# A graph block on one core: byte matrices written in runs of ten, keys summed against normed rows, and a new order around the seams

## The chip, the cores and the metric

The kernel runs on one core of a Trainium2 chip. The engines are TensorE (PE, with its weight loads shown apart as PEld), VectorE (DVE), ScalarE (ACT), GpSimd (POOL) and SyncE (SP), which here only issues transfers. Each engine works through its own list of instructions in order. The metric is the device time of one execution in microseconds (us), and times are medians over several runs.

## What is computed

There are 6250 nodes with 256 features and 200000 edges, sorted by their target (dst). Cut to what matters, the reference is:

```
xn = layernorm(x)
# graph convolution with self-loops: h = xn @ W, messages scaled by dinv[src] * dinv[dst]
gnn = relu(segment_sum((xn @ W)[src] * norm, dst) + b)
# linear attention mixer: q, k, v = xn @ Wqkv, 8 heads of 32
q, k = elu(q) + 1, elu(k) + 1
kv = einsum('nshd,nshm->nhmd', k, v);  ksum = k.sum(1)
t  = q . kv / (q . ksum + 1e-6)
x1 = layernorm(t + xn);  mix = layernorm(gelu(x1 @ W1 + b1) @ W2 + b2 + x1)
x  = x + gnn + mix
# 8 experts, one per token (argmax), at most 977 tokens each, in order of token
x  = x + expert_ffn(layernorm(x))      # 256 -> 1024 -> 256, times the gate's probability
```

The sums kv and ksum run over all nodes, so the second half of the mixer can start only when the keys of all nodes are done.

## The kernel before

Nodes are handled in 49 tiles of 128 rows (the last has 106), mostly two tiles at a time (25 "pairs"). There are three stages.

**First stage.** Two generators of instructions are woven together by hand: C, the chain of lists (`first_chain`), and F, the first passes over x (`first_passes`). Before the weaving starts, the statistics of the first eight tiles are placed (`all_of(x_stats(8))`). Then one step of C is followed by steps of F until F has made FIRST = 0.79 steps for each step of C. The order so made is the order on every engine.

C first finds where each node's edges begin (`search`): 25 comparisons of dst against the node numbers on DVE (L433), summed by PE (L436), give a coarse place per group of nodes (L447), then POOL fetches windows of dst (L454), in which DVE and ACT count (L466, L470). It needs dst alone, except that it pulls the statistics of x along. From the degrees follows dinv. Then C scales the rows of x in place (L403), splits them into a high and a low part in a table in SBUF (`tab`, L394 and L396) and writes them to memory (g_dram), and beside that builds the edge lists. At its end it adds up a few checks (`checked`).

F, per pair: ACT makes the normed rows (L682) out of x, which for the first NX = 6 pairs is read where it was loaded, and for the others is loaded once more (L673); PE turns them (L242); queries (L708), `ex` and `re` (elu + 1) and a write to memory (q_dram); then per tile keys and values in one product of 512 columns (L721), elu + 1 of the keys (L726, L728, L732), a copy of the values beside a column of ones (L730), and the outer product of keys and values, 129 columns for each half of the keys, summed in PSUM over all tiles (L694). It also fills the experts' buffer with zeros (L660, L661). Float32 products show as two records each in the profile, fp32r and bf16 ones as one.

After both, DVE masks the summed outer products by head (kvb), and a flag from the checks is loaded into all engines; a branch on it leads to a slow general path, which is not taken with these inputs.

**Aggregation.** Three generators are woven: `gather` (618 steps: 18 node tiles whose edges' rows POOL gathers from memory, L984, and PE adds up by one-hot products, L1002), `dense` (31 node tiles, in 13 steps each), and `rounds` (the rest of the block per pair, up to routing), which makes SIDE = 1.25 steps for each step of `gather`. A round waits for the sums of its pair.

`dense` counts edges in a matrix of 128 targets by 6272 sources per node tile. One-hot products (L967) give, in PSUM, 10 targets by 49 blocks of sources at a time; ACT casts them to bytes (L969), 403 times, into a tile [128, 128, 49] (place of the source in its block on the partitions, target, block), that is, 490 bytes in a row. The multiplication with the table needs one block of sources at a time, [128, 128]: ACT takes seven blocks (`widened`, L927, 217 times), reading bytes that lie 49 apart, into fp32r, and PE multiplies (L952).

In `rounds`, `routing` works once for two pairs: among others a running count over tiles on DVE (`fore`, L1052), two steps later a product on PE that waits for it (L1056), and at the end POOL scatters each token with its scale and its row number, 514 floats, into the experts' buffer `xbuf` (L1083).

**Experts.** The memory of the earlier stages is given back, and each expert loads its weights (1 MB each, L1332 and L1334) and its tokens (L1338: four tiles, then three, then the rest), turns the tokens (L1351), and does its two products (L1367, L1377). DVE copies out the row numbers (`who`, L1343), ACT multiplies by the scale (L1380), and POOL scatters the rows to the output (L1395). The loads of the first two experts are issued ahead of the first product.

## Time and profile before

| | |
|---|---|
| time, median of 8 runs | 1853.55 us (1845.24 to 1857.96) |
| profiled execution | 1855.44 us, of which its span 1853.3 us |
| PE busy | 1503.6 us (81%), granted clock 0.904 |
| DVE, ACT, POOL busy | 1087.7, 1040.6, 772.6 us |
| DMA | 286.41 MB, mean 155 GB/s |

A busy time is the time in which an engine has an instruction in work; PE's ends are modelled. The span is cut here by what the engines do: the first stage runs until 273 us, where the last outer product ends; the aggregation from the first one-hot at 281 us until the last table product at 1478 us; the last round and its routing follow, and the experts from 1518 us on.

### The profile page before, as it was taken

How to read it: one execution, taken by the hardware profiler on the slowest of the kernel's cores; microseconds unless marked ns; L12 is line 12 of the kernel's file. 1: busy time of each engine (PE TensorE's matmuls, PEld its weight loads, DVE VectorE, ACT ScalarE, POOL GpSimd, SP SyncE). 2: the span in 40 equal slices, each digit the busy share in tenths (PEclk: the TensorE clock that was granted, in tenths of full speed). 3: DMA queues.
4: the chain of work that ended last, by engine and by line, in shares of the span. 5: the costliest groups of instructions: out<-in, count | busy, mean ns of one | idle time of the engine just before them, and what ended most of it. 6: DMA issues, size and time to landing. Idle time of an engine off the chain costs nothing. (4 is left out here: it accounts for less than half of the span.)

```text
span 1853.3 us, 23596 instructions
## 1 busy us (share of the span) xinstructions
PE 1503.6 (81%) x7678; PEld 1085.5 (59%) x7678; DVE 1087.7 (59%) x3430; ACT 1040.6 (56%) x1639; POOL 772.6 (42%) x771
## 2 busy tenths in 40 slices
PE   4887786887877887888778888788888739999997
PEld 2554454665655665666556666566656526777775
DVE  4765856676676577667666767666766322223323
ACT  1844554767666676677557666666766413242332
POOL 0103506556546565555555555555655411111111
PEclk9988996999889998899889898888988859999999
DMA  7546787657556566565656565565665462332330
GB/s 224 152 123 190 240 265 183 161 154 189 141 155 161 153 169 178 145 168 149 169 155 166 148 169 159 148 159 159 156 158 143 119 221 103 104 108 102 109 105 21
DMA packets 184985, 286.41 MB, mean 155 GB/s; under 512 B 28457, under 2 KB 78564, under 8 KB 184714
## 3 DMA queue, kind: packets, MB, share of 16 engines
q0 software_dynamic: 96304, 180.15, 37.7%
q1 hardware_dynamic: 88250, 103.44, 17.1%
q8 instruction: 69, 1.13, 0.2%
q10 hardware_dynamic: 288, 1.08, 0.1%
q14 instruction: 74, 0.61, 0.1%
HBM read 226.90 MB, written 60.39 MB: 155 GB/s over the span
## 5 line engine op out<-in xcount | busy, mean ns | idle before, releaser
L984 POOL DMA_INDIRECT gt<-g_dram,idxc x612 | 622.5, 1017 | 548.4 <-PE ps L1002 296.5
L952 PE MATMUL ps_d<-tab,A_r 128*128 128x512 f32 x1519 | 453.7, 423 | 36.2 <-ACT A_r L927 25.7
L927 ACT CAST A_r<-A 128x896 fp32r<-128x896 uint8 x217 | 391.5, 1804 | 78.2 <-PE ps_d L952 50.2
L952 PEld LDWEIGHTS ps_d<-tab,A_r 128*128 128x128 f32 x1519 | 309.5, 205 | 116.8 <-ACT A_r L927 36.7
L969 ACT CAST A<-bp 128x490 uint8<-128x490 f32 (+1 forms) x403 | 221.1, 562 | 258.8 <-PE bp L967 133.4
L1002 PE MATMUL ps<-gt,oh 128*128 128x512 f32 x612 | 287.0, 504 | 6.8 <-DMA gt<-g_dram,idxc 5.8
L899 DVE TENSOR_TENSOR lo<-rowb,lo 128x640 bf16<-128x640 bf16 (+1 forms) x403 | 193.5, 480 | 137.0 <-PE bp L967 48.4
L967 PE MATMUL bp<-hi,lo 128*128 128x98 bf16 x1984 | 169.0, 217 | 41.8 <-DVE hi L899 20.3
L967 PEld LDWEIGHTS <-lo 128*128 128x128 bf16 x1984 | 108.3, 103 | 159.2 <-issue 86.1
L993 DVE TENSOR_TENSOR oh<-rowb,rel 128x256 fp32r<-128x256 bf16 x306 | 128.2, 419 | 106.0 <-PE ps L1002 73.4
L1395 POOL DMA_INDIRECT out<-rep,who x43 | 42.4, 986 | 300.7 <-DVE rep L1393 202.0
L899 DVE TENSOR_TENSOR hi<-hib,hi 128x490 bf16<-128x490 bf16 (+1 forms) x403 | 163.1, 405 | 0.0
L1367 PE MATMUL hpf<-xet,w1e 128*128 128x512 f32 (+2 forms) x544 | 151.5, 436 | 5.6 <-ACTq L1407 3.5
L1377 PE MATMUL ypf<-w2e,hm 128*128 128x256 f32 (+1 forms) x688 | 151.3, 379 | 0.0
L1377 PEld LDWEIGHTS ypf<-w2e,hm 128*128 128x128 f32 (+1 forms) x688 | 128.9, 188 | 21.9 <-issue 3.1
L1002 PEld LDWEIGHTS ps<-gt,oh 128*128 128x128 f32 x612 | 117.6, 208 | 13.6 <-DMA gt<-g_dram,idxc 6.1
L1367 PEld LDWEIGHTS hpf<-xet,w1e 128*128 128x128 f32 x544 | 85.5, 191 | 65.3 <-issue 57.4
L1369 ACT ACTIVATE hm<-hpf,fb_s 128x512 f32<-128x512 f32 (+2 forms) x136 | 71.0, 525 | 78.4 <-PE hpf L1367 73.9
L1379 DVE TENSOR_TENSOR y<-ypf,fb_s 128x256 f32<-128x256 f32 (+1 forms) x43 | 18.2, 423 | 140.1 <-PE ypf L1377 140.1
L721 PE MATMUL mm<-wqkv_s,xnt 128*128 128x512 f32 (+1 forms) x196 | 98.8, 629 | 0.0
L1380 ACT ACTIVATE y<-y,xe 128x256 f32<-128x256 f32 (+1 forms) x43 | 21.9, 508 | 119.4 <-DVE y L1379 119.4
L1206 ACT ACTIVATE s<-s,nb,rs 128x256 f32<-128x256 f32 (+1 forms) x98 | 53.5, 595 | 49.5 <-DVE nb L1200 18.9
(307 smaller groups left out, 2074.3 us busy)
## 6 DMA issues: line engine op xcount, KB each, us to landing
g_dram<-tab SPq DMA_DIRECT2D x24, 512.0 KB
xt<-in_x SPq DMA_DIRECT2D x42, 256.0 KB
xbuf<-zeros SPq DMA_DIRECT2D x26, 384.0 KB
gt<-g_dram,idxc POOLq DMA_INDIRECT x612
xe<-xbuf SPq DMA_DIRECT2D x8, 1028.0 KB
w1e<-in_fw SPq DMA_DIRECT2D x8, 1024.0 KB
w2e<-in_fw SPq DMA_DIRECT2D x8, 1024.0 KB
xe<-xbuf SPq DMA_DIRECT2D x8, 771.0 KB
```

The costliest lines, as they stand in the source:

```text
L721: nc.tensor.matmul(kp[:r, :], xnt[:, c, i * r:i * r + r], wqkv_s[:, c, D:3 * D], start=(c == 0), stop=(c == 1))
L899: V.tensor_tensor(one[:, :g1 - g0, :].rearrange("p g (w t) -> p g w t", t=2), row.rearrange("p (w t) -> p w t", t=2).unsqueeze(1).to_broad ...
L927: nc.scalar.copy(o, mats[u][:, :, c * CH:(c + 1) * CH].rearrange("p n s -> p s n"))
L952: nc.tensor.matmul(acc_ps, parts[u - 1, hi // CH][:, hi % CH, :], source(hi), start=False, stop=(hi == NB - 1))
L967: nc.tensor.matmul(bp[:, g * HI:(g + 1) * HI], lo[:, g, :], hi[:, g, :], start=(g == 0), stop=(g == g1 - g0 - 1))
L969: nc.scalar.copy(mats[u][:, GN * g0:GN * g1, :].rearrange("p n s -> p (n s)"), bp[:, :(g1 - g0) * HI])
L984: nc.gpsimd.indirect_dma_start(out=gt, out_offset=None, in_=g_dram, in_offset=bass.IndirectOffsetOnAxis(ap=idxs[j // IC][:, j % IC:j % IC ...
L993: V.tensor_tensor(oh, rowb.unsqueeze(1).to_broadcast([P, 2, P]), rel[:, m:m + 2].unsqueeze(2).to_broadcast([P, 2, P]), op=OP.is_equal)
L1002: nc.tensor.matmul(ps, ohs.pop(i), tiles.pop(i), start=False, stop=(e == EB - 1))
L1367: nc.tensor.matmul(hp[:, :nn], w1e[:, c, f * P:(f + 1) * P], xet[:, c, at:at + nn], start=(c == 0), stop=(c == 1))
L1369: nc.scalar.activation(hm[:, f, :nn], hp[:, :nn], AF.Relu, bias=fb1_s[:, e * 8 + f:e * 8 + f + 1])
L1377: nc.tensor.matmul(yp[:r, :], hm[:, f, (i - i0) * P:(i - i0) * P + r], w2e[:, f, :], start=(f == 0), stop=(f == DFF // P - 1))
```

## The change

- **Bytes.** The byte matrix becomes [128, 49, 128] (place in the block, block, target). The cast out of PSUM (L969 before) reads 10 values that lie 49 words apart and writes them as a run of ten bytes, 49 runs for one cast; the widening cast (L927 before) reads seven blocks in a row.
- **Mixer sums.** F multiplies keys alone (256 columns, two tiles in one bank), so that exp, relu and elu + 1 of the keys are one operation each per pair. The outer product is taken of keys with the normed rows and a column of ones (257 columns, `kx_ps`, two banks). After the last pair the sum is copied, turned, multiplied with the values' weights, and masked. Normed rows have three buffers of their own and are made two pairs ahead; the turn of the next pair stands in F's first step. F has three steps per pair instead of five.
- **Order of the first stage.** The first nine steps of C (ALONE) stand ahead of the statistics of the first eight tiles. FIRST is 0.465. x is read in place for 18 pairs, so 7 pairs instead of 19 are loaded again.
- **Flag and first loads.** The checks are added up when C ends, and the flag is loaded two steps of F later. The loads of the first two rounds are made by a function of their own, `load_round`; it is called for them twice. In the order that results, on every engine the branch comes right behind F, and the turning and multiplying of the sum stands behind the branch, ahead of the aggregation's first one-hots.
- **Routing** has one step more between the running count and the product that needs it. SIDE is 1.28.
- **Experts** live where the table was (`big` now outlasts the stages): weights in its first two parts, tokens in the next two, the middle layer in the last two. The first expert's weights are asked for as soon as `gather` and `dense` are done. Tokens come ahead of weights, for the first expert tile by tile; scales and row numbers come by loads of their own, 8 bytes a row (`xm`).

```
-SIDE = 1.25
-NX = 6
-FIRST = 0.79
+SIDE = 1.28
+NX = 18
+ALONE = 9
+FIRST = 0.465
...
-    kv_ps = kps.tile([P, 2, 132], F32, name="kv_ps")
+    kx_ps = kps.tile([P, 2, 512], F32, name="kx_ps")
     cr_ps = rps.tile([P, 512], F32, name="cr_ps")
-    sm_ps = rps.tile([P, 512], F32, name="sm_ps")
+    sm_ps = cr_ps[:, 128:]
...
-            xn = pair("S", 2, "xn")
+            xn = xns[gi % 3]
...
-        def outer(t, r, ek, va):
-            for g in range(2):
-                nc.tensor.matmul(kv_ps[:, g, :129], ek[:r, g * P:(g + 1) * P], va[:r, g, :],
-                                 start=(t == 0 and g == 0), stop=(t == NB - 1 and g == 1))
+        def outer(gi, ek):
+            t0, n = twos[gi]
+            r = rows(t0)
+            for i in range(n):
+                for g in range(2):
+                    nc.tensor.matmul(kx_ps[:, g, :D + 1], ek[:r, i, g * P:(g + 1) * P], xns[gi % 3][:r, i, :],
+                                     start=(t0 + i == 0), stop=(t0 + i == NB - 1))
...
-            re = pair("G", 3, "re")
+            re = pair("S", 2, "re")
             nc.scalar.activation(re[:, :, :nn], qp[:, :, :nn], AF.Relu)
-            xn = normed(gi + 1) if gi + 1 < NGR else None
+            if gi + 1 < NGR:
+                turned(gi + 1, xns[(gi + 1) % 3])
             yield
             V.scalar_tensor_tensor(ex[:, :, :nn], ex[:, :, :nn], 1.0, re[:, :, :nn], op0=OP.min, op1=OP.add)
             nc.sync.dma_start(q_dram[gi, :, :, :nn], ex[:, :, :nn])
+            kp = bank().rearrange("p (t o) -> p t o", t=2)
             for i in range(n):
-                kp = bank()
                 for c in range(2):
-                    nc.tensor.matmul(kp[:r, :], xnt[:, c, i * r:i * r + r], wqkv_s[:, c, D:3 * D],
+                    nc.tensor.matmul(kp[:r, i, :], xnt[:, c, i * r:i * r + r], wqkv_s[:, c, D:2 * D],
                                      start=(c == 0), stop=(c == 1))
...
+            if late:
+                outer(*late.pop())
+            ek = rw.tile([P, 2, D], F32, name="ek", tag="ek", bufs=2)
+            nc.scalar.activation(ek[:r, :n], kp[:r, :n], AF.Exp)
+            rk = pair("S", 2, "rk")
+            nc.scalar.activation(rk[:r, :n], kp[:r, :n], AF.Relu)
+            if gi + 2 < NGR:
+                normed(gi + 2)
+            yield
+            V.scalar_tensor_tensor(ek[:r, :n], ek[:r, :n], 1.0, rk[:r, :n], op0=OP.min, op1=OP.add)
+            late.append((gi, ek))
+            yield
...
+    def load_round(k):
+        if k < len(twos):
+            gi = order[k]
+            t0, n = twos[gi]
+            r = rows(t0)
+            round_x[gi] = pair("X", 3, "xt")
+            nc.sync.dma_start(round_x[gi][:r, :n, :], node_rows(x, t0, n))
+            round_q[gi] = pair("Q", 2, "q")
+            nc.sync.dma_start(round_q[gi][:, :, :n * r], q_dram[gi, :, :, :n * r])
...
+        for _ in range(ALONE):
+            next(C)
+        all_of(x_stats(8))
+        while any(live):
+            if live[1]:
+                live[1] = next(C, "end") != "end"
+                c += 1
+                if not live[1]:
+                    badi = judged()
+                    asked = f + 2
+            while live[0] and (f < FIRST * c or not live[1]):
+                live[0] = next(F, "end") != "end"
+                f += 1
+                if not live[1] and f == asked:
+                    flag = nc.values_load(badi[0:1, 0:1], min_val=0, max_val=1)
+        assert f > asked
+        for k in range(2):
+            load_round(k)
+
+        kx = pair("S", 2, "kx")
+        nc.scalar.copy(kx, kx_ps[:, :, :D])
+        kxt = pair("S", 2, "kxt").rearrange("p c (g m) -> p c g m", g=2)
+        tp = bank()
+        for g in range(2):
+            V.tensor_scalar(kvb[:, g, 128:132], hmask[:, :, 0], kx_ps[:, g, D:D + 1], None, op0=OP.mult)
+            for c in range(2):
+                nc.tensor.transpose(tp[:, (2 * c + g) * P:(2 * c + g + 1) * P], kx[:, g, c * P:(c + 1) * P], ident)
+        nc.scalar.copy(kxt.rearrange("p c g m -> p (c g m)"), tp)
+        kv = bank()
+        for g in range(2):
+            for c in range(2):
+                nc.tensor.matmul(kv[:, g * P:(g + 1) * P], kxt[:, c, g, :], wqkv_s[:, c, 2 * D + g * P:2 * D + (g + 1) * P],
+                                 start=(c == 0), stop=(c == 1))
+            V.tensor_tensor(kvb[:, g, 0:128], kv[:, g * P:(g + 1) * P], hmask.rearrange("p a b -> p (a b)"), op=OP.mult)
+        for k in range(2):
+            load_round(k)
...
-                    nc.scalar.copy(o, mats[u][:, :, c * CH:(c + 1) * CH].rearrange("p n s -> p s n"))
+                    nc.scalar.copy(o, mats[u][:, c * CH:(c + 1) * CH, :])
...
-                        mats[u] = de.tile([P, P, NB], U8, name="A", tag="A")
+                        mats[u] = de.tile([P, NB, P], U8, name="A", tag="A")
...
-                        nc.scalar.copy(mats[u][:, GN * g0:GN * g1, :].rearrange("p n s -> p (n s)"), bp[:, :(g1 - g0) * HI])
+                        nc.scalar.copy(mats[u][:, :, GN * g0:GN * g1],
+                                       bp[:, :(g1 - g0) * HI].rearrange("p (n s) -> p s n", s=NB))
...
             yield
+            yield
             yield
             pp = bank()
...
+            if not (alive["g"] or alive["d"] or weights):
+                weights.append(weights_of(0))
...
-            for i0, i1 in ((0, 4), (4, NCT - 1)):
+            parts = [(i, i + 1) for i in range(4)] if e == 0 else [(0, 4)]
+            for i0, i1 in parts + [(4, NCT - 1)]:
                 nc.sync.dma_start(xe[:, i0:i1, :],
-                                  xbuf[r0 + i0 * P:r0 + i1 * P, :].rearrange("(t p) d -> p t d", p=P))
...
+            w1e, w2e = weights.pop() if e == 0 else weights_of(e)
+            nc.sync.dma_start(xm[:, :NCT - 1, :], xbuf[r0:i1, 2 * D:].rearrange("(t p) d -> p t d", p=P))
+            nc.sync.dma_start(xm[:last, NCT - 1, :], xbuf[i1:r0 + CAP, 2 * D:])
```

## The prediction

> **What bounds the kernel now.** I read the windows of busy time by stage first, then who waits for whom in the longest stage, then the groups of instructions by shape, then the order of time at the seams. By stage (start and end, length, then busy us and count on PE, its weight loads, DVE, ACT and POOL, granted clock, DMA share, GB/s):
>
> ```profile
> 0.00:23.00 23.00, 0.00 (x0) 0.08 (x1) 11.65 (x78) 1.69 (x2) 3.21 (x18) 1.00 0.77 237
> 23.00:50.00 27.00, 25.46 (x109) 12.58 (x108) 12.09 (x30) 9.03 (x22) 0.00 (x0) 1.00 0.69 203
> 50.00:145.00 95.00, 80.18 (x315) 51.76 (x314) 71.19 (x276) 59.92 (x162) 6.92 (x7) 0.91 0.44 133
> 145.00:273.00 128.00, 101.31 (x406) 66.04 (x406) 85.15 (x248) 72.27 (x181) 43.88 (x42) 0.91 0.77 246
> 273.00:282.00 9.00, 0.07 (x1) 0.01 (x1) 1.51 (x8) 0.49 (x2) 0.00 (x0) 0.54 0.17 45
> 282.00:1478.00 1196.00, 973.28 (x5462) 720.64 (x5462) 800.30 (x2512) 786.59 (x1055) 670.59 (x656) 0.89 0.61 159
> 1478.00:1520.00 42.00, 8.85 (x36) 6.78 (x36) 11.16 (x55) 2.83 (x6) 5.60 (x5) 0.59 0.55 195
> 1520.00:1853.00 333.00, 314.48 (x1355) 227.58 (x1353) 94.62 (x228) 107.74 (x211) 42.39 (x43) 0.99 0.28 97
> ```
>
> Four parts: the lists and the first passes (0 to 273), PE idle for 23 us and 81% busy from 50 on; aggregation (282 to 1478), where PE is 81%, DVE 67% and ACT 66% busy, so none is full and each waits in its own order for the others; a tail (to 1520) in which the routing's last scatter and the first load of tokens stand alone; the experts, PE 94% busy at clock 0.99. In the aggregation PE waited (us in total, times, longest):
>
> ```profile
> PE mm L242 <- ACT s L1206: 31.2, 16, 4.3
> PE mm L1056 <- DVE fore L1052: 28.6, 11, 3.5
> ...
> PE ps_d L952 <- ACT A_r L927: 25.7, 18, 5.9
> ...
> PE mm L1238 <- ACT x1t L1220: 7.9, 5, 2.5
> ```
>
> The groups that the change touches there, with two DVE rows for comparison (busy us, mean ns; the tile's row of L886 has min/median/max ns):
>
> ```profile
> L927 ACT CAST A_r<-A 128x896 fp32r<-128x896 uint8 x217 | 391.5, 1804 | 78.2 <-PE ps_d L952 50.2 <-remote 11.7 <-PE bp L967 10.0
> L969 ACT CAST A<-bp 128x490 uint8<-128x490 f32 x372 | 206.5, 569 | 214.0 <-PE bp L967 104.7 <-PE ps L1002 46.1 <-remote 44.8
> ```
>
> ```profile
> L886 DVE TENSOR_REDUCE ag<-ps_d x31: 682/691/692, 342.8 to 1478.0; 128x256 f32<-128x512 f32 x31
> ```
>
> ```profile
> L1281 DVE TENSOR_TENSOR s<-mm,s 128x512 f32<-128x512 f32 x24 | 16.5, 687 | 8.4 <-PE mm L1272 8.4
> ```
>
> L927, reading bytes 49 apart, costs 1804 ns for 896 elements; L394, a contiguous ACT cast of 512 elements, costs 628.
>
> **The change, part by part.** The sum is made against the profiled execution, 1855.4 us (span 1853.3); the median shown is 1.9 lower.
>
> *First stage, head.* From the order of time:
>
> ```profile
> 15.80 0.43 DVE L374 BATCH_NORM_STATS2 six<-x_in 128x6 f32<-128x256 f32 x1 [9.58 <-DMA x_in<-in_x]
> ...
> 22.79 0.76 DVE L433 TENSOR_SCALAR lt<-reps,lastf 125x784 bf16<-125x784 int16 x2
> 23.27 2.14 PE L436 MATMUL et_ps<-lt,oneb 125*1 125x448 bf16 x6 [23.27 <-DVE lt L433]
> ```
>
> ```profile
> 50.05 0.17 DVE L447 TENSOR_SCALAR at<-cr_ps 112x7 f32<-112x7 f32 x1 [2.43 <-PE cr_ps L445]
> ```
>
> The search needs only dst, whose loads are issued before those of x. When they land no view shows: between 2.5 us (issue) and 15.8 (x, behind them, was there). I take 8: dst's 0.8 MB stand ahead of the first 1 MB of x, and 237 GB/s move both in 7.6. 25 steps at the 0.7 us that six matmuls in 2.14 show end at 25; then DVE has its copy (0.6) and, now ahead of L447, eight tiles of statistics (6.8 from 15.8 to 22.6): L447 at 33 instead of 50, 17 us earlier.
>
> *First stage, work per pair of tiles.* From rows at 252 to 256 us:
>
> ```profile
> 254.07 1.88 PE L721 MATMUL mm<-wqkv_s,xnt 128*128 128x512 f32 x4
> ```
>
> ```profile
> 252.34 1.89 PE L708 MATMUL mm<-xnt,wqkv_s 128*128 128x256 f32 x8
> ...
> 255.78 0.61 PE L694 MATMUL kv_ps<-va,ek 128*128 128x129 f32 x4
> ```
>
> Keys and values cost PE 2 x 1.88 per pair; keys alone are eight records of 256 columns, as L708: 1.89. The outer product grows from 129 to 257 columns: from 2 x 0.61 to some 1.89. Net -1.20 per pair, x 24.5 pairs = -29 us of PE, on the path: at the 81% that PE keeps from 50 on, -36. ACT loses six operations of 0.38 and gains two of 0.60 per pair (-27 in all), DVE's two of 0.42 become one of 0.69 (-4): beside PE, counted at nothing. Twelve loads of x (256 KB, 1.04 us of SP each) go; SP and DMA (0.77 busy) are not named by PE's waits, so nothing again, and if C's rows were short of them it is a gain. Against that: before, 1.5 pairs were done by 50 us, now none by 33: 1.5 x 6.2 / 0.81 = +12. And in the order of the changed program three pairs of F stand behind the end of the chain of lists, with nothing beside them: +6. In place of the row reads (x_in) DVE's in-place scaling (L403) waits for ACT's norms; these stand two pairs ahead in the order, so 0.
>
> *Seam.* 9 us lie between the last products and the first one-hot (273 to 282): flag load, branch, a barrier. The flag is now read two F steps after it is made (its load was 0.7 us). But the summed keys-times-norms must be copied, turned, copied, multiplied and masked before DVE's first one-hot: ACT 0.6, PE 0.6, ACT 0.6, PE 0.6, DVE 0.6, with handovers some 4; of this the old mask and check (1 us) and the load go away: +2. SP loads the first two rounds twice; the second set waits for the first set's buffers, and the round behind it needs them only after the chain: 0, at most 3.
>
> First stage: -17 - 36 + 12 + 6 + 2 = -33. Bounds: -3, if the chain of lists sets its end (-17 + 2.7 pairs x 6.2 alone at the end - 3 at the seam), and -45, if neither lost pairs nor lone pairs cost.
>
> *Aggregation.* L927 now reads contiguous bytes. From 256 to 512 elements ACT's copies go from 383 to 608 ns (L730, L690), 0.88 ns an element; 896 give 628 + 384 x 0.88 = 0.97 us. Bounds 0.97 and 1.80 (should the cast itself be slow; but L910 widens 128 bytes in 0.31). I take 0.97: -0.84 x 217 = -182 us of ACT's 787. L969 now reads PSUM at steps of 49 words and writes runs of ten bytes, 403 times. Bounds: 0.57, as now, and 1.07, if each of 490 elements costs what L927's do now. The nearest row by memory is L886: neighbouring reads there are 256 words apart, and its 691 ns equal L1281's 687 of contiguous PSUM. It is DVE, not ACT; still I take 0.57.
>
> [...]
>
> What reaches PE: the 18 waits for A_r shrink by up to 0.84 each: -15. The 31 waits for ACT's s, x1t, ht and agt (31.2 + 7.9 + 5.5 + 4.4 = 49.0) shrink, where a cast stands ahead, by half of that: -13. The routing's extra step: 618 gather steps in 1196 us with 1.25 round steps each make 1.55 us a step; the 11 waits for fore lose that: -17. SIDE 1.28 for 1.25 moves round steps 2% earlier; they wait for sums: 0. Together -45. Bounds: -17 (ACT buys nothing) and -95 (nearly all of the 79 us that ACT's groups end, and the fore waits). What is late next: DVE (hi, lo and ag end 40 us of PE's waits).
>
> *Tail and experts.* The last scatter took 7.10 us while 4 MB of weights were in flight (issued 1492.8 to 1501.6); these now go out near 1478 and are gone by then: 0 to -4, taken -2.5. Tokens took 5.39 us as 1 MB and come tile by tile: 0 to -5, taken -2.5. Later experts load tokens ahead of weights, and their scales and row numbers (8 bytes a row) last, behind 4 MB issued 27 us before use: DVE's who waits for them with PE's next products not behind it; 0, and if they come late, 2 us for each of six experts.
>
> Sum: 1855.4 - 33 - 45 - 5 = 1772; less 1.9, **1770**.
>
> **Rivals.**
> 1. *L969 pays for its strided read* (1.07): +206 us of ACT cancel L927's -182, and ACT's -28 is gone: 1798. For it: L927's own price. Against: L886.
> 2. *The chain of lists sets the first stage's end*, -3 instead of -33: 1800. For it: DVE is 67% busy from 145 on and the chain has DMA round trips (L449 to L466). Against: PE's 81% in the same stretch.
> 3. *ACT is the pacemaker of the aggregation*: -95 instead of -45: 1720. For: 79 us of PE's waits end on ACT. Against: ACT itself waits more for PE (105 us at L969 alone) than PE for it.
> 4. *Slower: L969 at 1.8 us*, strided read and short runs both paying. ACT then has 787 - 182 + 403 x 1.23 = 1101 us; at 88% busy the stage takes 1250, +54, which less 38 elsewhere gives 1871 (1869). It decides from 1.76 us on. Against: no ACT row costs over 2.0 ns an element, this would be 3.7.
> 5. *The cast is slow, not the stride*: L927 stays at 1.80: 1798. Against: L910, L394.
>
> **Numbers.** Chances: forecast 0.51, rivals 0.20, 0.10, 0.08, 0.07, 0.04. Runs of the kernel before differ by 0.7%, medians of several by less; 0.3% is about what tells a change from none. Rivals 1 to 3 and 5 are faster; 4 is slower. Of the 0.93 of the faster cases I give 0.02 to no change and 0.01 to slower, for several misses at once: faster 0.90. The range runs from rival 3 to rival 1 or 2 with something of the other: 1722 to 1818; left out are rival 4, both of 1 and 2, and the far side of 3, some 0.15. The forecast's own range is 1750 to 1792.
>
> **What would show it.** Right: L447's counterpart at 31 to 37 us; last outer product near 240; first one-hot near 249; the A_r cast at 0.97 and the A cast at 0.57; waits for fore near 1 us each; aggregation near 1150 long; first token transposes some 35 us after its end. Wrong, above all, if the A cast comes out at 1 us or more, or if the chain of lists ends the first stage later than 250.

## The result and the profile after

The changed kernel took 1835.35 us (median of 12 runs, 1824.68 to 1843.59), the kernel before 1851.91 in the same comparison (33 runs): ratio 0.991, 95% interval 0.989 to 0.993. The forecast was 1770 with a range of 1722 to 1818, so the sign was right and four fifths of the gain did not come: 83 us were forecast (1853.55 - 1770), 16.6 came. The profiled execution took 1833.1 us, span 1831.2.

In some comparisons the kernel before took 1852 to 1856 us (called here the first condition), in others 1731 to 1734 (the second), and one and the same chip showed both, so a ratio is taken within one comparison and traces are compared within one condition. The traces of before and after are of the first, the pair c_before and c_after further below of the second.

The stages of the changed kernel, first condition (start and end, length, then busy us and count on PE, its weight loads, DVE, ACT and POOL, granted clock, DMA share, GB/s):

```profile
0.00:23.00 23.00, 7.53 (x29) 2.67 (x30) 11.66 (x66) 1.28 (x1) 3.21 (x18) 1.00 0.77 234
...
36.00:126.00 90.00, 70.37 (x310) 58.17 (x310) 69.25 (x265) 56.88 (x126) 6.95 (x7) 0.87 0.41 126
126.00:241.00 115.00, 85.47 (x371) 70.56 (x372) 76.56 (x218) 61.30 (x124) 43.81 (x42) 0.87 0.76 241
241.00:264.00 23.00, 18.47 (x85) 15.29 (x83) 8.75 (x22) 8.19 (x18) 0.00 (x0) 0.93 0.60 191
...
272.40:1451.80 1179.40, 973.82 (x5462) 722.92 (x5462) 800.79 (x2513) 615.49 (x1055) 672.38 (x656) 0.89 0.63 164
1451.80:1489.00 37.20, 8.16 (x28) 5.72 (x28) 10.67 (x54) 2.50 (x5) 5.62 (x5) 0.54 0.28 94
1489.00:1831.20 342.20, 318.38 (x1360) 229.32 (x1360) 92.89 (x221) 108.32 (x211) 42.50 (x43) 0.97 0.30 99
```

The early marks came earlier, the first of them about as forecast: the search ends at 35.5 us (forecast 33), the row weights stand at 126.0 instead of 145.3, and the chain of lists ends at 240.4 instead of 266.0. But the last outer product ends at 263.6 instead of 273.0: for 23 us F runs alone behind the chain, where it was 7 before. The first one-hot comes 9.0 us earlier. ACT lost 171 us of work in the aggregation (786.6 to 615.5), which got 17.4 us shorter, PE's own 973 us being the same. The tail up to the first product of an expert is 0.7 shorter, and the experts from that product on are 5.0 longer (338.0). The sum is -9.0 - 17.4 - 0.7 + 5.0 = -22.1, the difference of the spans.

The two casts came out as the forecast took them (ACT's groups in the aggregation):

```profile
L1023 ACT CAST A<-bp 128x490 uint8<-128x490 f32 x372 | 217.0, 590 | 317.2 <-PE bp L1021 157.7 <-PE ps L1057 70.8 <-remote 51.9
L981 ACT CAST A_r<-A 128x896 fp32r<-128x896 uint8 x217 | 204.1, 941 | 83.1 <-PE ps_d L1006 49.3 <-remote 19.7 <-PE ps L1057 7.3
```

L981 at 941 ns (forecast 970, before 1804), L1023 at 590 (569 before). PE's waits in the aggregation, and two of ACT's (us in total, times, longest):

```profile
...
PE mm L243 <- ACT s L1250: 33.2, 16, 5.5
...
PE mm L1112 <- DVE fore L1107: 18.1, 10, 2.5
...
PE mm L1211 <- ACT agt L1184: 12.3, 7, 3.5
PE ps_d L1006 <- ACT A_r L981: 10.1, 6, 2.7
```

```profile
ACT A L1023 <- PE bp L1021: 185.0, 121, 5.8
...
ACT s L1250 <- DVE nb L1244: 54.4, 16, 7.0
```

The wait for A_r fell by 15.6 us, as forecast, and the one for fore by 10.5 where 17 were forecast. The wait for s did not fall (31.2 before): ACT itself waits there, 54.4 us, for DVE's nb. What ACT gave up became idle time of ACT.

### The profile page after: what moved, and what is told of

It reads as the page before. It is cut to its first block, busy times and chain, and to the rows that moved or that the text cites. A ratio compares the mean times of both kernels' runs of the same rounds, so it can differ in the third digit from the quotient of the medians.

```text
span 1831.2 us, 23437 instructions
## 1 busy us (share of the span) xinstructions
PE 1492.0 (81%) x7690; PEld 1110.0 (61%) x7690; DVE 1082.7 (59%) x3399; ACT 856.4 (47%) x1544; POOL 774.7 (42%) x771
## 3 DMA queue, kind: packets, MB, share of 16 engines
q1 hardware_dynamic: 93846, 101.04, 17.1%
## 5 line engine op out<-in xcount | busy, mean ns | idle before, releaser
L1006 PE MATMUL ps_d<-tab,A_r 128*128 128x512 f32 x1519 | 454.4, 424 | 23.4 <-issue 13.1
L1023 ACT CAST A<-bp 128x490 uint8<-128x490 f32 (+1 forms) x403 | 231.8, 581 | 369.7 <-PE bp L1021 185.0
L1006 PEld LDWEIGHTS ps_d<-tab,A_r 128*128 128x128 f32 x1519 | 309.8, 205 | 98.3 <-issue 17.8
L953 DVE TENSOR_TENSOR lo<-rowb,lo 128x640 bf16<-128x640 bf16 (+1 forms) x403 | 193.8, 481 | 125.6 <-PE ps L1057 41.0
L981 ACT CAST A_r<-A 128x896 fp32r<-128x896 uint8 x217 | 204.1, 941 | 83.1 <-PE ps_d L1006 49.3
L953 DVE TENSOR_TENSOR hi<-hib,hi 128x490 bf16<-128x490 bf16 (+1 forms) x403 | 163.1, 405 | 0.0
L1418 PE MATMUL hpf<-xet,w_e 128*128 128x512 f32 (+2 forms) x544 | 154.3, 441 | 8.5 <-ACTq L1459 3.5
L1428 PE MATMUL ypf<-w_e,hm 128*128 128x256 f32 (+1 forms) x688 | 151.3, 379 | 0.0
L1428 PEld LDWEIGHTS ypf<-w_e,hm 128*128 128x128 f32 (+1 forms) x688 | 128.8, 188 | 22.0 <-issue 3.8
L1418 PEld LDWEIGHTS hpf<-xet,w_e 128*128 128x128 f32 x544 | 86.7, 194 | 70.5 <-issue 62.2
L1250 ACT ACTIVATE s<-s,nb,rs 128x256 f32<-128x256 f32 (+1 forms) x98 | 53.5, 594 | 74.1 <-DVE nb L1244 54.4
L1431 ACT ACTIVATE y<-y,xm 128x256 f32<-128x256 f32 (+1 forms) x43 | 21.8, 508 | 134.4 <-DVE y L1430 132.2
L1139 POOL DMA_INDIRECT xbuf<-slot,put x48 | 51.6, 1075 | 67.1 <-issue 42.9
```

Source lines behind the costliest of these rows:

```text
L953: V.tensor_tensor(one[:, :g1 - g0, :].rearrange("p g (w t) -> p g w t", t=2), row.rearrange("p (w t) -> p w t", t=2).unsqueeze(1).to_broad ...
L981: nc.scalar.copy(o, mats[u][:, c * CH:(c + 1) * CH, :])
L1006: nc.tensor.matmul(acc_ps, parts[u - 1, hi // CH][:, hi % CH, :], source(hi), start=False, stop=(hi == NB - 1))
L1023: nc.scalar.copy(mats[u][:, :, GN * g0:GN * g1], bp[:, :(g1 - g0) * HI].rearrange("p (n s) -> p s n", s=NB))
L1418: nc.tensor.matmul(hp[:, :nn], w1e[:, c, f * P:(f + 1) * P], xet[:, c, at:at + nn], start=(c == 0), stop=(c == 1))
L1428: nc.tensor.matmul(yp[:r, :], hm[:, f, (i - i0) * P:(i - i0) * P + r], w2e[:, f, :], start=(f == 0), stop=(f == DFF // P - 1))
```

## The experiments

### The lone end of the first passes: e1_first

```diff
-FIRST = 0.465
+FIRST = 0.505
```

> The changed kernel with FIRST 0.505 in place of 0.465: in the order of the program some four or five steps of the first passes are left when the chain of lists ends, instead of eleven. Theory (the lone tail): in the changed kernel the chain of lists ended at 240.4 us and the last outer product at 263.7, and those 23 us ate the gain of the first stage; here the chain ends at 245 to 250 and the last outer product at 254 to 258, -6 to -10 us, about 1827 us, 0.987 of the kernel before. Rival (the stage is full all the same, what moves out of the tail lengthens the stretch ahead of it one for one): chain end near 252, last outer product 262 to 265, time 1833 to 1837, ratio 0.990 to 0.992.

Measured in the second condition: ratio 0.981 (0.977 to 0.985), the changed kernel 0.983 there (c_after, below). The chain of lists ended at 246.8 us instead of 236.8, the last outer product at 259.6 instead of 260.0, the first one-hot at 267.2 instead of 268.6. The rival was right in kind: what moves out of the lone end lengthens the stretch ahead of it almost one for one.

### The layout of the bytes: e2_layout and b_layout

Undone in the changed kernel:

```diff
-nc.scalar.copy(o, mats[u][:, c * CH:(c + 1) * CH, :])
+nc.scalar.copy(o, mats[u][:, :, c * CH:(c + 1) * CH].rearrange("p n s -> p s n"))
...
-mats[u] = de.tile([P, NB, P], U8, name="A", tag="A")
+mats[u] = de.tile([P, P, NB], U8, name="A", tag="A")
...
-nc.scalar.copy(mats[u][:, :, GN * g0:GN * g1],
-               bp[:, :(g1 - g0) * HI].rearrange("p (n s) -> p s n", s=NB))
+nc.scalar.copy(mats[u][:, GN * g0:GN * g1, :].rearrange("p n s -> p (n s)"), bp[:, :(g1 - g0) * HI])
```

> The changed kernel with the byte matrix laid out as before (49 bytes between neighbours for the A_r cast, contiguous writes for the A cast): ACT gets some 182 us back in the aggregation, all else stays. The forecast's terms (18 waits for A_r x 0.84 = 15, other waits for ACT 13): aggregation 1207 instead of 1179, time 1863, ratio 1.006. Theory now (ACT was not what PE waited for, its relief became ACT idle time): aggregation +4 to +12, time 1839 to 1847, ratio 0.993 to 0.997. Rival (the layout alone made the whole gain of the aggregation): +17, 1852, ratio 1.000.

The same lines the other way round in the kernel before, nothing else:

> The kernel before with the new layout of the byte matrix alone (both casts), nothing else changed. Theory (the layout is the whole gain of the change where the standstills are gone; undone in the changed kernel it cost 29 us): aggregation 25 to 36 shorter than 1079, ratio 0.979 to 0.986. Forecast's terms for ACT (15 + 13): 28 shorter, ratio 0.984. Rival (it pays only together with the other edits of the aggregation): under 15, ratio above 0.991.

Measured: e2_layout 0.999 (0.997 to 1.002), second condition; against 0.983 of the changed kernel there, the layout is worth 0.0169 x 1732 = 29 us, with an uncertainty of 6 from the two intervals. b_layout 0.987 (0.983 to 0.991), first condition: 24 us, uncertain by 7. The forecast's 28 stands, and the theory made from the first pair of traces (4 to 12 us) falls. Within the errors the layout is the whole gain: in the first condition it gives 0.987 alone, where the whole change gives 0.991, and the aggregation with it alone is 1177.2 us long (279.6 to 1456.8) against 1179.4; in the second condition nothing is left without it.

### The routing's extra step: e3_route

```diff
                 V.tensor_add(fore[:, b + 1, :], fore[:, b, :], oh[:, b, :])
             yield
             yield
-            yield
             pp = bank()
```

> The changed kernel without the routing's extra step: the product over fore is issued one step of the rounds earlier. Forecast (each of 11 waits loses 1.55 us): PE's wait for fore grows from 18.1 back to 28 us or more and the time by 17: 1852, ratio 1.000. Theory now (named waits fell by 10 only, and some of that came back at other waits): +3 to +8, ratio 0.993 to 0.995. Rival (the step buys nothing, a wait only moves to the next one): within 2 us of the changed kernel, ratio 0.990 to 0.992.

Measured: 0.976 (0.972 to 0.980) against 0.983, so without the step the kernel is 11 us faster, uncertain by 8. PE's wait for fore is 20.2 us (11 times) without the step and 18.8 (11 times) with it, and 23.6 in e2_layout, which has the step and the old layout. The step does next to nothing for the wait that it was to shorten; forecast (17 us worse) and theory (3 to 8 worse) are both wrong. The traces do not show the 11 us either: the profiled executions of the two kernels took 1699.3 and 1700.7 us, as close as the rival had it.

### The distance from DVE to ACT to PE in the rounds: e4_norms

```diff
                 V.scalar_tensor_tensor(nb, mstat[:, :, 0], -1.0, rs, op0=OP.mult, op1=OP.mult)
                 yield
                 yield
+                yield
+                yield
```

> The changed kernel with two more steps of the rounds between the DVE chain that ends in nb and ACT's norms. In the changed kernel ACT waited 54.4 us for nb and PE 33.2 us for the s that these norms write (16 times each). Theory (PE's waits in the rounds are the distance from DVE to ACT to PE in the written order, not the load of any engine): both waits fall below 15 us, the aggregation shortens by 12 to 25 us, time 1811 to 1823, ratio 0.978 to 0.985. Rival (the engines are late by their load, so the wait shows up at the next handover): the wait for s falls, others grow as much, aggregation within 5 us, ratio 0.988 to 0.994. Second rival (25 rounds that are two steps longer make the tail longer): -5 to +5 with the tail some 3 us longer.

Measured: 0.962 (0.959 to 0.965), 36 us below the changed kernel, uncertain by 7: in this condition two empty steps are worth about as much as the whole change (30 us). PE's waits in the aggregation of e4_norms, then ACT's:

```profile
PE ps L1057 <- DMA gt<-g_dram,idxc: 32.2, 32, 4.1
PE bp L1021 <- DVE hi L953: 19.8, 11, 2.7
PE mm L1112 <- DVE fore L1107: 13.5, 11, 2.6
...
PE mm L243 <- ACT s L1252: 6.2, 5, 2.2
```

```profile
ACT A L1023 <- PE bp L1021: 264.0, 202, 6.0
...
ACT s L1252 <- DVE nb L1244: 28.1, 18, 3.2
```

In c_after these two waits were:

```profile
PE mm L243 <- ACT s L1250: 51.1, 37, 3.9
```

```profile
ACT s L1250 <- DVE nb L1244: 71.5, 25, 4.5
```

The aggregation of e4_norms (columns as in the stages above):

```profile
271.30:1278.90 1007.60, 893.98 (x5454) 671.35 (x5454) 795.64 (x2510) 614.19 (x1055) 681.09 (x656) 0.95 0.72 193
```

It is 1007.6 us long instead of 1046.5 (-38.9). PE idles only 11.9 less: the wait for s fell by 44.9, but the waits for gathered rows and for hi grew (14.6 to 32.2 and 8.7 to 19.8). The other 27.0 is PE's busy time (894.0 against 921.0, the same 5460 or so records), and most of that is the clock. In these traces the granted clock is either 1.0 or 0.5, and by the records of it PE lost 62 us of its busy time to half clock in c_after and 39 in e4_norms. In c_after most products with x1t took 379 ns at 1.0, and most of those at 0.5 some 634; in the first trace of the changed kernel these are the medians of the 125 that ran at 1.0 throughout and of the 62 at 0.5. Why less of the time is at half clock is not shown.

So the theory holds for the wait for s, which is a distance in the written order, and not for the wait for nb, which did not fall below 15 (28.1). The first rival is right for most of the idle time, which moved to the next handovers, and the larger part of the gain was in neither. The second rival fell: a round that is two steps longer cost next to nothing (the tail is 0.5 us longer), as a round waits in the written order until the sums of its pair are there.

### Both kernels in the second condition: c_before and c_after

Nothing is edited; the first pair had shown times in which PE, DVE and ACT stood still together, some 35 us of the aggregation in each trace.

> The kernel before, unchanged, once more with its trace: the four kernels above ran on another chip than the first two traces, with the kernel before at 1731.5 us there instead of 1852. In the traces of the first chip PE, DVE and ACT stood still together for 35 us of the aggregation with no releaser that the trace shows, in both kernels; in the traces of the other chip for 0 to 5 us. Theory (the standstills belong to the chip, not to the change): here too they are gone, the first stage is as long as on the first chip within 6 us (270 to 282 to the first one-hot), the aggregation is 1060 to 1080 instead of 1197. Rival (the changed kernel's order removes them): the kernel before shows 20 us of them here too.

> The changed kernel, unchanged, beside the kernel before on one chip, with both traces. Theory (where the standstills are gone, the layout of the bytes is worth what the forecast gave it, 28, or the 36 by which the aggregation of the kernel with the old layout was longer; the rest of the change is worth little): aggregation 1030 to 1040, ratio 0.976 to 0.982. Rival (the ratio of the first chip holds everywhere): 0.989 to 0.993.

Measured: c_after 0.983 (0.980 to 0.985), at 1700.7 us against 1733.8. Counting stretches over 0.1 us, PE, DVE and ACT stood still together for 0.1 us of the aggregation in c_before and for 2.2 in c_after, against some 35 in each trace of the first pair. So the standstills do not come from the change. Nor do they belong to a chip, as those expectations supposed: the chip of e1 to e4, 1731.5 us then, later gave 1855.75 for the same kernel, with 31 to 45 us of them in three traces. The stages, c_before then c_after:

```profile
0.00:23.00 23.00, 0.18 (x1) 0.16 (x2) 12.08 (x79) 2.13 (x3) 3.21 (x18) 1.00 0.81 242
23.00:50.00 27.00, 25.55 (x113) 13.01 (x112) 12.19 (x32) 8.69 (x22) 0.03 (x1) 1.00 0.80 207
50.00:144.00 94.00, 80.34 (x310) 51.59 (x308) 70.69 (x276) 59.88 (x162) 6.90 (x7) 0.91 0.45 131
144.00:258.00 114.00, 92.80 (x379) 60.69 (x380) 79.55 (x231) 69.85 (x173) 43.62 (x42) 0.94 0.84 263
258.00:265.00 7.00, 5.40 (x29) 3.34 (x27) 5.93 (x18) 2.54 (x8) 0.00 (x0) 1.00 0.81 224
...
272.70:1351.40 1078.70, 934.30 (x5462) 699.47 (x5462) 799.98 (x2513) 785.41 (x1056) 673.61 (x656) 0.92 0.68 177
1351.40:1395.10 43.70, 10.61 (x37) 7.81 (x36) 10.99 (x55) 3.09 (x6) 5.60 (x5) 0.57 0.54 190
1395.10:1728.40 333.30, 314.51 (x1353) 227.82 (x1352) 94.43 (x228) 107.67 (x210) 42.41 (x43) 0.99 0.28 96
```

```profile
0.00:23.00 23.00, 7.08 (x27) 2.54 (x28) 11.20 (x64) 1.28 (x1) 3.21 (x18) 1.00 0.78 228
23.00:36.00 13.00, 7.07 (x38) 3.25 (x37) 11.08 (x39) 0.43 (x1) 0.00 (x0) 0.86 0.86 270
36.00:126.70 90.70, 70.48 (x310) 58.24 (x310) 69.77 (x268) 57.25 (x126) 6.93 (x7) 0.87 0.44 125
126.70:236.80 110.10, 81.99 (x366) 67.70 (x367) 76.72 (x217) 60.26 (x122) 44.01 (x42) 0.91 0.82 249
236.80:260.00 23.20, 19.61 (x89) 16.39 (x87) 9.32 (x23) 9.00 (x19) 0.00 (x0) 0.92 0.66 203
...
268.60:1315.10 1046.50, 921.01 (x5462) 688.91 (x5462) 799.29 (x2513) 615.31 (x1055) 675.31 (x656) 0.93 0.71 185
1315.10:1355.30 40.20, 9.94 (x37) 6.50 (x37) 10.58 (x54) 3.15 (x7) 5.62 (x5) 0.58 0.37 121
1355.30:1698.80 343.50, 318.43 (x1352) 229.49 (x1352) 92.62 (x221) 107.65 (x210) 42.41 (x43) 0.97 0.30 95
```

The sum: first one-hot -4.1, aggregation -32.2, tail -3.5, experts +10.2, together -29.6, the difference of the spans. In the first stage (up to the last outer product) PE has 186.2 us of work instead of 204.3, and idles 73.8 instead of 60.7: of 18.1 us that were taken from PE, 13.1 came back as idle time. The head shows how: PE idled 24.3 of the first 50 us before, and idles 21.9 of the first 36 now, so that an end of the search 13 us earlier takes 2.4 us of idle time away.

### The search ahead of x: e5_search

```diff
-ALONE = 9
-FIRST = 0.465
+ALONE = 0
+FIRST = 0.437
```

> The changed kernel with the search not ahead but beside the first passes, as before (ALONE 0, statistics of eight tiles first, FIRST 0.437 so that the same steps of the first passes are left at the end of the chain). Theory (the head's 17 us were no saving, since PE ran 25.5 of the 27 us from 23 to 50 in the kernel before, with pairs of the first passes in them): the search ends 10 to 15 us later, but 1.5 pairs are done by then, the last outer product ends within 4 us of the changed kernel's and the time is within 4 us of it. Forecast (17 earlier, 12 lost with the overlap): 5 us slower. Rival (the chain of lists sets the stage's end): 10 to 15 us slower.

Measured: 0.983 (0.980 to 0.986), as the changed kernel. The search ends at 44.3 us instead of 36.1, the last outer product at 264.8 instead of 260.0, the first one-hot at 273.9 instead of 268.6. At the end of the stage the earlier search is worth 5 us, what the forecast's 17 less 12 gave; in these two traces the aggregation gives it back (1039.4 against 1046.5).

### Scales and row numbers apart from the tokens: e6_tokens

```diff
-xe = big.tile([P, NCT, 2 * D], F32, name="xe", tag=f"T{2 + e % 2}")
-xm = fw.tile([P, NCT, 2], F32, name="xm", tag="xm")
+xe = big.tile([P, NCT, ROW], F32, name="xe", tag=f"T{2 + e % 2}")
+xm = xe[:, :, 2 * D:]
...
-nc.sync.dma_start(xm[:, :NCT - 1, :], xbuf[r0:i1, 2 * D:].rearrange("(t p) d -> p t d", p=P))
-nc.sync.dma_start(xm[:last, NCT - 1, :], xbuf[i1:r0 + CAP, 2 * D:])
```

> The changed kernel with a token's scale and row number loaded in one row with it, as before, instead of by two loads of 8 bytes a row behind the weights. In the changed kernel the experts took 338.0 us from the first product instead of 333.0, with a wait of PE of 3.0 to 6.7 us at the branch of the last experts (PE's queue, L1457) that the kernel before does not show. Theory A (small packets are in the way of what PE's queue waits for): that wait and the 3 to 5 us go, time -3 to -6. Theory B (the wait comes with the code's place and has nothing to do with the loads): within 2 us of the changed kernel, the wait stays.

Measured: 0.984 (0.982 to 0.986), the changed kernel's 0.983 within the error; the wait at the branch is still there (3.5 us, once, as in the first trace of the changed kernel), so theory A falls. The last expert of c_before, and of c_after, in PE's order of time (PEq and ACTq are the sequencers of PE and ACT, under which the traces list waits for semaphores and branches: L1405 ACTq COMPARE_BRANCH x8, 40 ns by the median in the first trace of the kernel before):

```profile
1690.95 3.27 PE L1367 MATMUL hpf<-xet,w1e 128*128 128x512 f32 x7 [0.68 <-ACTq L1405]
```

```profile
1658.93 3.75 PE L1418 MATMUL hpf<-xet,w_e 128*128 128x512 f32 x4 [3.20 <-PEq L1457]
```

Where an expert has no more than four tiles, PE jumps over the blocks for more. In c_after that jump cost 3.4 and 3.2 us instead of 0.7, twice, and the 32 products behind it took 15.6 and 16.5 us instead of 14.0: (3.4 + 3.2 - 1.4) + (1.6 + 2.5) = 9.3 of the 10.2 us. During the last of these waits two transfers of instructions run, one behind the other (16 KB from 1656.1, 8 KB from 1658.0), as in the one long wait of the changed kernel's first trace, 3.04 us until PE goes on at 1791.35 (16 KB from 1788.7, 8 KB from 1790.7); in c_before the only one begins at 1690.9, as PE goes on. The long wait shows once or twice in 12 of the 13 traces of the changed kernel and what was built on it (not in d_double), and in one of the four of the kernel before (n3_double, once). The same program has it once (after) and twice (c_after). So the loads are not needed for it; what decides between 0.7 and 3 us stays open.

### The price of PE's work in the first stage: d_double and n3_double

d_double does the key product of the changed kernel twice:

```diff
-for c in range(2):
+for c in (0, 1, 0, 1):
     nc.tensor.matmul(kp[:r, i, :], xnt[:, c, i * r:i * r + r], wqkv_s[:, c, D:2 * D],
                      start=(c == 0), stop=(c == 1))
```

> The changed kernel with the key product of the first passes done twice into the same bank (start flag set again, so the result is the same): eight more records of PE per pair, 24.5 x 1.9 to 2.2 = 46 to 54 us of PE in the first stage. Forecast (PE's work there is on the path, divided by the share of 0.81 that PE keeps): first one-hot 57 to 65 later than in the changed kernel, ratio 1.015 to 1.020. Theory now (PE is 72% busy in the first stage of the changed kernel and waits in its order for DVE and ACT, so that much of its work lies in those waits): 20 to 40 later, ratio 0.994 to 1.006. Rival (the chain of lists alone sets the stage): under 10 later.

n3_double does the keys' half of the product once more in the kernel before:

```diff
+for c in range(2):
+    nc.tensor.matmul(kp[:r, :D], xnt[:, c, i * r:i * r + r], wqkv_s[:, c, D:2 * D],
+                     start=(c == 0), stop=(c == 1))
```

> The kernel before with the keys' part of the product over keys and values done once more (eight records of 256 columns per pair, 46 to 54 us of PE in the first stage). Forecast's price for PE's work in this stage (each us divided by PE's share of 0.81): first one-hot 57 to 65 later, ratio 1.031 to 1.037. Theory now (0.5 to 0.65 us for each us of PE, as in the changed kernel, where 34 us more of PE put the end off by 22): 20 to 30 later, ratio 1.010 to 1.017.

Both in the first condition. d_double: 0.998 (0.995 to 1.000). Up to its last outer product, at 285.8 us:

```profile
0.00:285.80 285.80, 226.75 (x1024) 184.91 (x1024) 179.18 (x608) 128.19 (x269) 52.18 (x67) 0.91 0.59 183
```

n3_double: 1.011 (1.007 to 1.015). Up to its last outer product, at 286.5 us:

```profile
0.00:286.50 286.50, 238.85 (x1024) 163.57 (x1024) 180.67 (x629) 144.39 (x366) 54.89 (x67) 0.96 0.64 193
```

The changed kernel had 188.4 us of PE up to 263.6, so 38.4 us more of PE put the end off by 22.2: 0.58 us for each. The kernel before had 207.0 up to 273.0, so 31.9 us more put it off by 13.5: 0.42 for each. The forecast charged 1.23 (one over PE's share of 0.81). Less busy time was added than the 46 to 54 us expected, in part because the granted clock of the stretch was higher with the added work (0.91 against 0.88 in the changed kernel, 0.96 against 0.92 in the kernel before). The first one-hot of n3_double came 15.3 us later, where the theory had 20 to 30.

### What holds the late stretch: d_early

```diff
-z0, z1 = (nz * k // (NGR - 1) for k in (gi, gi + 1))
-blanks(*((z0, z1 - z0) if gi < NGR - 1 else (nz, 1)))
+z0, z1 = (nz * min(k, 8) // 8 for k in (gi, gi + 1))
+if gi == NGR - 1 or z1 > z0:
+    blanks(*((z0, z1 - z0) if gi < NGR - 1 else (nz, 1)))
```

> The changed kernel with the zero rows of the tokens' buffer (16 MB) written beside the first eight pairs of the first passes instead of all 24. DMA was 0.44 busy from 36 to 127 us and 0.82 from 127 to 237 in the changed kernel. Theory (the late stretch of the first stage is held by transfers: rows of the lists come late, DVE and PE wait for them): DMA below 0.7 there, the chain of lists ends 8 to 15 us earlier than at 237, first one-hot 5 to 12 earlier, ratio 0.976 to 0.980. Rival (the order of PE, DVE and ACT holds it): within 3 us of the changed kernel everywhere, ratio 0.981 to 0.984.

Measured in the first condition: 0.988 (0.984 to 0.992) against the changed kernel's 0.991. DMA was 0.57 busy from 127 to 240 us instead of some 0.76, and 0.87 from 36 to 127; the chain of lists ended at 239.8 (240.4), the first one-hot came at 272.1 (272.4). The rival was right: transfers do not hold this stage.

### Reading x in place, and the mixer alone: n1_reload and n2_mixer

n1_reload:

```diff
-NX = 18
+NX = 6
```

> The changed kernel with x read in place for 6 groups only (NX 6, as before), the other 18 loaded again. Theory A (reading in place ties the chain of lists to the first passes: DVE scales the rows in place behind ACT's norms): the chain and the first one-hot come 6 to 12 us earlier. Forecast (in place buys and costs nothing): within 3 us. Rival (in place saves transfers that hold the stage): 4 to 10 later. The first one-hot of the changed kernel was at 268.6 and 272.4 us on the two kinds of chip, ratios 0.9825 and 0.9911.

n2_mixer has ALONE = 0, NX = 6 and FIRST = 0.437:

> The changed kernel with its first stage as before but for the mixer: search beside the first passes (ALONE 0, FIRST 0.437), NX 6. What is left of the change ahead of the aggregation is the sum of keys times norms, pair by pair, and the seam. Against the kernel before (first one-hot 272.7 and 279.6 to 281.4 on the two kinds of chip): forecast, -36 of PE's work and +2 of the seam, 34 earlier. Theory now (18 us of PE less at 0.65 us for each, +2 of the seam): 8 to 12 earlier. Rival (the first passes, now in longer operations per pair, hand over more slowly and give all of it back): within 4 us of the kernel before.

Both in the first condition. n1_reload: 0.989 (0.984 to 0.993), first one-hot at 273.0 (the changed kernel 272.4): reading in place buys and costs nothing, as forecast. n2_mixer: 0.989 (0.984 to 0.993), last outer product at 273.1, first one-hot at 281.3, the kernel before 273.0 and 281.4. PE had 189.8 us of work up to that point instead of 207.0 and idled 17 us more. The rival was right: in this order the mixer's sums, with 17 us less of PE, give nothing at the end of the stage. At 0.42 to 0.58 us each they should have given 7 to 10; the chain of lists does end 17 us earlier (248.6 against 266.0), and F then runs alone for 24.5 us instead of 7. Why F, with less work, is not earlier is not shown.

### A version that beats both: best

The edits of e1_first, e3_route and e4_norms together.

> The changed kernel with three edits: two more steps between the DVE chain that ends in nb and ACT's norms (alone 0.962), the routing's extra step undone (alone 0.976), FIRST 0.505 (alone 0.981; the changed kernel 0.982). If the gains add: 0.954 to 0.958. If the routing's step was luck of the runs: 0.960 to 0.963.

Measured in the first condition: 1789.2 us, 0.965 (0.960 to 0.969), where the changed kernel gives 0.991. That is less than either range, both of which add up gains of the second condition. The aggregation is 1132.6 us long (269.0 to 1401.6) instead of 1179.4. Whether the routing's edit adds to e4_norms can't be read from it: e4_norms ran only in the second condition.

## Why the prediction was wrong, by its steps

By stage, -33, -45, -5 and 0 were forecast for the first stage, the aggregation, the tail and the experts. Measured were -9.0, -17.4, -0.7 and +5.0 in the first condition and -4.1, -32.2, -3.5 and +10.2 in the second.

- **First stage, work per pair (-36 forecast): the step that failed most.** The price was wrong: dividing by PE's busy share supposes that PE's idle time grows with its work, while waits in the written order can take work in or let it go. The price measured by putting work in is 0.42 to 0.58, not 1.23. And less came than was forecast: from one undisturbed pair the forecast took 1.20 us a pair, 29 in all; PE's busy time fell by 18.6 (207.0 to 188.4; 18.1 in the second condition), and in n2_mixer by 17.1. The pair itself was not far off. With the part that went to half clock taken out, by the clock records of the two traces, PE's work fell by 24.6 (190.7 to 166.1), but the granted clock of the stage fell too, from 0.92 to 0.88. At the measured price 18.6 us were worth 8 to 11, and alone (n2_mixer) they gave nothing.
- **Head and lost overlap (-17 + 12): about right as a sum**, 5 us at the stage's end in e5_search, and 9 in the first condition, where n2_mixer and n1_reload differ by the same edit (273.1 and 264.0). The 17 by itself was never a saving, since PE worked 25.5 of the 27 us from 23 to 50 before.
- **Lone pairs (+6).** The forecast gives no working for this term. The lone stretch grew by 16 us, not 6 (23 instead of 7), but e1_first shows that this is a place in the order and no cost: evened out, it gives 1.4 us back. **Seam (+2):** 8.4 before, 8.8 after. **x in place (0):** right.
- **Stage as a whole: -33 forecast, -9 and -4 measured.** By these traces, one of each kernel, what came is the search ahead of x. In the first condition the last outer product ends at 273.0 before, 273.1 with the mixer's sums (n2_mixer), 264.0 with the search moved ahead as well (n1_reload) and 263.6 with x in place; in the second at 264.9 before, 264.8 without the search moved (e5_search) and 260.0 with it. Two slips in the forecast's sums changed nothing: its bound of -45 (neither lost nor lone pairs cost) is -51 by its own terms, and rival 1's +206 is about 201.
- **Aggregation, ACT's casts (-15 - 13): right in size, by luck in the split.** 29 and 24 us by e2_layout and b_layout. The forecast took 15 from the waits for A_r and 13 from those for s, x1t, ht and agt. In the first pair the wait for A_r fell by 15.6, but the other four together grew (49.0 to 54.9). In the second condition, from e2_layout to c_after, the wait for A_r had only 4.7 us to give, and the other four fell by 22 (agt 13.7 to 5.9, x1t 13.9 to 7.4, ht 2.3 to under 1, s 57.3 to 51.1); PE's busy time fell by 10 too, which the forecast held fixed. The wait for s, the largest, was for the most part never ACT's load: it is the distance from DVE to ACT to PE, by e4_norms. In the first pair the aggregation gives 17 and not 28; a pair of single traces in the first condition has 35 us of standstills in each kernel, and which waits they hide was not tested.
- **Aggregation, routing (-17): wrong.** The wait did shrink in both pairs (28.6 to 18.1, 28.7 to 18.8), which looks like the forecast, but e3_route shows nearly the same wait without the step. Eleven waits were priced by the step's length, although no row said that fore was late by the order rather than by DVE.
- **Tail (-5): right up to the first token transposes, not behind them.** Up to these it is 2.8 and 5.7 us less, but the first expert's product comes 3.9 us behind the first transposes instead of 1.8, so that 0.7 and 3.5 are left. **Experts (0): wrong.** 5.0 and 10.2 us more, by a jump of which no row before told.
- **The rivals.** 1, 4 and 5 fell with the first reading of the casts. 3 asked for PE to gain more than ACT's measured waits and fell too. 2 named about the right size for the first stage (-3) by a cause that the trace does not show: the chain of lists ended 23 us ahead of the stage's end.

On the casts, what the stride costs was measured on either side of the change (c_before and c_after). ACT's read of bytes 49 apart in SBUF pays: 1811 ns against 940 in a row for 896 elements. ACT's read of words 49 apart in PSUM does not, beyond some 18 ns: 571 against 589 for 490 elements, the write in runs of ten bytes included. For the second the forecast followed the row of L886, rightly.

## What to carry to other kernels

Where no engine is full, a stage's idle time is not a tax on the busiest engine's work: price work there by putting some in (here 0.42 and 0.58 us for each), not by dividing by the busy share (1.23). Busy time moves with the granted clock (a product with x1t took 379 ns at 1.0 and 634 at 0.5), so look at the clock before reading a change of busy time as a change of work. A wait for ACT's result is worth a faster ACT only if ACT is busy ahead of it; if ACT itself waits for DVE, the cure is distance in the written order, which here was two empty steps (PE's wait for s went from 51.1 us to 6.2). A wait that shrinks as forecast does not prove the forecast's reason; undo that one edit (the wait for fore: 18.8 us with the step, 20.2 without).

## What was not expected of the hardware

Standstills of three engines at once. In the first condition PE, DVE and ACT stop together, in the trace of the kernel before for up to 3.4 us at a time and 35 us of the aggregation, and for most of that time (28 of the 35 us) what ends it is given as "remote" or "issue", nothing in the trace. From the order of time of the kernel before:

```profile
701.56 1.04 ACT L969 CAST A<-bp 128x490 uint8<-128x490 f32 x2 [4.63 <-remote]
701.56 0.49 DVE L899 TENSOR_TENSOR lo<-rowb,lo 128x640 bf16<-128x640 bf16 x1 [4.21 <-remote]
701.83 1.03 POOL L984 DMA_INDIRECT gt<-g_dram,idxc  x1 [2.26 <-remote]
...
702.18 0.57 PE L967 MATMUL bp<-hi,lo 128*128 128x98 bf16 x5 [4.00 <-issue]
```

Of the eight longest stops in each of the two first traces, six of sixteen have a transfer of instructions within them or in the 6 us ahead; with 86 such transfers in the 1196 us before, that is no more than chance gives. The single operations of DVE and ACT take the same time in both conditions (DVE's L953 into lo 486 ns in the changed kernel's first trace and in e1_first, ACT's L1023 590 and 589), PE's are somewhat shorter in the second (L1006 424 ns in the changed kernel's first trace, 412 in e1_first). The cause is open.

The share of time at half clock. In these traces the granted clock is 1.0 or 0.5, and by the records of it PE lost 112 and 114 us of its busy time in the aggregation to half clock in the first two traces, 79 and 62 in c_before and c_after, and 39 in e4_norms. Without this loss PE's work there is 854 to 862 us in all five: what differs in PE's busy time is for the most part the clock.
